# An LSTM step over row pairs as two accumulated Strassen products, in a four-layer graph network

## The chip, the cores and the metric

The kernel runs on one core of one Trainium2 chip. The metric is the device time of one execution in microseconds (us), from the first instruction to the last. Three runs of the kernel before gave 2534.42, 2536.03 and 2541.12 us; the median, 2536.03 us, is the number to compare with.

A core has a matrix engine (TensorE, "PE" in a profile, with its weight loads as "PEld"), a vector engine (VectorE, "DVE"), an engine for activation functions (ScalarE, "ACT"), GpSimd ("POOL"), and SyncE ("SP"), which here only issues transfers. TensorE reads from the on-chip memory SBUF and writes its sums into PSUM, eight banks of 512 fp32 numbers for each of 128 partitions.

## The reference, cut to what matters

The input is 128 small graphs of 64 nodes with 256 features, so 8192 rows of 256 numbers, and one adjacency matrix of 64 x 64. Four graph layers follow one another, each of the form `x = layernorm(x + layer(x, adj))`. All is fp32. Layer 0 has three matrix products with the squared adjacency, layer 1 goes through the eigenvectors of a 64 x 64 matrix, layer 2 is two graph convolutions and then LSTMs along the nodes, layer 3 is attention. Only layer 2's LSTMs are changed:

```python
def step(carry, x_t):
    h, c = carry
    g = x_t @ Wih.T + h @ Whh.T + bias
    i, f, gg, o = jnp.split(g, 4, axis=-1)
    c = sigmoid(f) * c + sigmoid(i) * tanh(gg)
    h = sigmoid(o) * tanh(c)
    return (h, c), None
...
for p in range(1, MAX_SKIP + 1):            # 1, 2, 3, 4
    nw = Tv // p
    wins = h[:, :nw * p, :].reshape(Bv * nw, p, Hd)
    last = _lstm_last(Wih[p-1], Whh[p-1], bih[p-1], bhh[p-1], wins)
    h = h.at[:, arange(nw) * p + (p - 1), :].set(last.reshape(Bv, nw, Hd))
```

For p = 2 each window is a pair of neighbouring nodes. Its first step has a zero state, so only `x_t @ Wih.T` counts. Its second step needs both products: 1024 gate values (four gates of 256) from 256 features of x and 256 of h.

## The kernel before, in words

**Groups.** The 8192 rows are 64 tiles of 128 rows, taken four at a time: 16 groups of 512 rows, which are 8 graphs of 64 nodes. All rows stay in SBUF in one tile `X` (64 KB for each partition).

**Two phases.** In the first phase layer 0 runs over all groups, two at a time, while VectorE works out the eigenvectors (`eigen`) in between. At the end of each group of layer 0 the operations of its normalization are put in a list, `norms`, fourteen for each group; the matrix products of the following group take one from it each (`between`, and the loop over products in `layer0`). In the second phase `group(g)` takes each group through layers 1, 2 and 3 and writes it out; three groups (`WAYS`) are in flight.

**Order.** TensorE's order is written out by hand. Each group is a generator that yields the time at which its next matmul may start, by a clock `now` which adds up matmul costs. The loop at the end takes the oldest group that is due; if none is, it moves the clock on. The wait after a chain on other engines is a constant: after an LSTM step it is `CELL[n]`, 3.8 us for 256 columns. If the chain takes longer in truth, TensorE stands still, since it works strictly in order. The orders of VectorE and ScalarE are chosen by the tile scheduler, and they are kept in order too.

**LSTM steps.** `lstm(hT, p, first, nw)` holds the nodes transposed: `hT` has the 256 features as two halves k of 128 partitions, and as columns node and graph. For p = 2 there are 32 pairs in each of 8 graphs: n = 256 columns. A step makes 8 blocks, gate (f, i, g, o) by half h, each one PSUM bank: two matmuls with the 128 x 128 weight blocks of `wih` for the two k, and two with `whh` for the state `hs`. Each block then goes through a tanh on ScalarE (line 1030; sigmoids are tanh with a scale) to the SBUF tile `gates`. Lines 1034 to 1038 make c, line 1039 tanh(c), line 1041 the state of a step that is not the last, line 1051 the write of the last state into `hT`. In every step but the first, the x part of the first two blocks is given to TensorE ahead of the wait for the state (`early`, `ahead`).

For p = 3 and p = 4 the columns are 168 and 128, so matmuls of 128 columns are already in the kernel; p = 1 is taken in two halves of 256 columns.

**Buffers.** The pool `pw` has five tiles of 1024 columns with the tag "w" for `hT`, the mixed rows and layer 3's tiles; `pv` has four of 512; `psb` has the eight PSUM banks; `pg` holds gates, c and states three times.

Of the kernel before, what the change touches and what calls it, by code (L numbers as in the profile page):

```python
# [10 lines left out]
F32 = mybir.dt.float32  # L11
# [522 lines left out]
P = 128  # L534
# [3 lines left out]
ENDING = (14, 15)  # L538
LEAD = 10


def norm_parts(tc, pool, x, half, scalar=False):

# [53 lines left out]
def kernel(  # L597
# [46 lines left out]
    def load(pool, name, src, pattern, shape, **kw):  # L644
        t = pool.tile(shape, F32, name=name)
        nc.sync.dma_start(t, src.rearrange(pattern, **kw))
        return t

    X = keep.tile([P, NT, D], F32, name="X")
    adst = keep.tile([P, N], F32, name="adst")  # L650
    eig_c = ea.tile([P, len(CONSTS), N], F32, name="eig_c")
    nc.scalar.dma_start(adst[:N, :], adj)
    nc.sync.dma_start(adst[N:, :], adj)
    nc.scalar.dma_start(X[:, 2:4, :], x_t[:, 2:4, :])
    for t in range(2):
        nc.sync.dma_start(X[:, t, :], x_t[:, t, :])
# [6 lines left out]
    for t in range(4, NT, 2):  # L663
        nc.sync.dma_start(X[:, t:t + 2, :], x_t[:, t:t + 2, :])
    nc.sync.dma_start(eig_c, consts)

    ident = keep.tile([P, P], F32, name="ident")
# [74 lines left out]
            yield now[0] + 0.3  # L742

    def layer0(g):
        xs = X[:, 4 * g:4 * g + 4, :]

        def mixed(dst, src, nf, more, then=None):
            for c in range(nf):
# [105 lines left out]
        for t in (2, 0):  # L854
            p = tl(psa, [P, 2, D], "ps", bufs=6)
            mm(p, sqT2, s3[:, t:t + 2, :])
            yield now[0]
            x2 = xs[:, t:t + 2, :]
            VL.tensor_add(x2, p, x2)
            norms.extend(scalar_norm(tc, small, x2, half, spare))  # L860

# [50 lines left out]
    for i in range(4):  # L912
        wih.append(load(wb, f"wih{i}", c_ih[i], "(k p) f -> p k f", [P, 2, 1024], p=P))
        whh.append(load(wb, f"whh{i}", c_hh[i], "(k p) f -> p k f", [P, 2, 1024], p=P) if i else None)
    att = []
    for i in range(WAYS):
        att.append(wb.tile([P, 4, P], F32, name=f"att{i}"))
# [44 lines left out]
    def layer1(xs, ready):  # L962
# [25 lines left out]
            yield now[0]  # L988
        return ready

    def lstm(hT, p, first, nw):

        n = 8 * nw
        wi, wh, bias = wih[p - 1], whh[p - 1], cbi[:, p - 1, :]
        c = hs = None
        for t in range(p):
            rows = slice(first + t, first + t + (nw - 1) * p + 1, p)
            xt = [hT[:, k, rows, :] for k in range(2)]  # L1000
            last = t == p - 1
            names = "figo" if t else "igo"
            G = tl(pg, [P, 2048], "gates")[:, :2 * len(names) * n].rearrange("p (q h n) -> p q h n", h=2, n=n)
# [12 lines left out]
            if p > 1 and not t:  # L1016
                c = tl(pg, [P, 512], "c")[:, :2 * n].rearrange("p (h n) -> p h n", h=2)
            new = None if last else tl(pg, [P, 512], "hs")[:, :2 * n].rearrange("p (h n) -> p h n", h=2)
            for h, q in units:
                j = 2 * "ifgo".index(q) + h  # L1020
                m = slice(j * P, (j + 1) * P)
                pp = ahead.get((h, q))
                if pp is None:
                    pp = ps4()[:, :n]
                    for k in range(2):
                        mm(pp, wi[:, k, m], xt[k], k == 0, k == 1 and not t)
                if t:
# [12 lines left out]
                if q == "o" and not last:  # L1040
                    V.scalar_tensor_tensor(new[:, h, :], gate["o"][:, h, :], 1.0, gate["i"][:, h, :], op0=ALU.add,  # L1041
                                           op1=ALU.mult)
                if q == "o":
                    if h == 0:
                        yield now[0]
                elif h == 1 or len(units) == 8:
                    yield now[0]
            if last:

                for h in range(2):  # L1050
                    V.scalar_tensor_tensor(hT[:, h, slice(first + p - 1, first + nw * p, p), :],  # L1051
                                           gate["o"][:, h, :].rearrange("p (w b) -> p w b", b=8), 1.0,
                                           gate["i"][:, h, :].rearrange("p (w b) -> p w b", b=8), op0=ALU.add,
                                           op1=ALU.mult)
            ready = now[0] + CELL[n]
            hs = new
        return ready

    def layer2(xs, g, ready):
        a = yield from mixed(xs, adT2, ready)  # L1060
        g1 = as3(work(), 4)
        ready = []
        for t in range(0, 4, 2):
            p = ps4((P, 2, D))
            for j in range(2):
                run(p[:, j, :], [(a[:, k, (t + j) * P:(t + j + 1) * P], cw0[:, k, :]) for k in range(2)])
            V.tensor_add(g1[:, t:t + 2, :], p, wide["c_b0"].unsqueeze(1).to_broadcast([P, 2, D]))
            relu(g1[:, t:t + 2, :], g1[:, t:t + 2, :])
            ready.append(now[0] + CONV)
            yield now[0]  # L1070
        a = yield from mixed(g1, adT2, ready)
        hT = tl(pw, [P, 1024], "w").rearrange("p (k n b) -> p k n b", k=2, b=8)
        for c in range(2):
            p = ps4((P, 4, P))
            run(p, [(cw1[:, k, c * P:(c + 1) * P], a[:, k, :]) for k in range(2)])
            h = work2()
            V.scalar_tensor_tensor(as3(h, 4), rs_row.unsqueeze(1).to_broadcast([P, 4, P]), cb1[:, c:c + 1], p,
                                   op0=ALU.mult, op1=ALU.add)
            S.activation(hT[:, c, :, :].rearrange("p n b -> p b n"), as3(h, 8), AF.Relu, scale=2.0)
            yield now[0]  # L1080
        ready = now[0] + CONV
        for p, first, nw in ((1, 0, 32), (1, 32, 32), (2, 0, 32), (3, 0, 21), (4, 0, 16)):
            if first == 0:
                yield ready
            ready = yield from lstm(hT, p, first, nw)
        hb = as3(work(), 2)
        V.tensor_copy(as3(hb[:, 0, :], 8), hT[:, 0, :, :].rearrange("p n b -> p b n"))
        S.copy(as3(hb[:, 1, :], 8), hT[:, 1, :, :].rearrange("p n b -> p b n"))
        yield ready + 1.6
        ready = []  # L1090
        for t in range(0, 4, 2):
            p = ps4((P, 2, D))
            for j in range(2):
                for k in range(2):
                    turn(p[:, j, k * P:(k + 1) * P], hb[:, k, (t + j) * P:(t + j + 1) * P])
            V.scalar_tensor_tensor(xs[:, t:t + 2, :], p, 0.5, xs[:, t:t + 2, :], op0=ALU.mult, op1=ALU.add)  # L1096
            norm(xs, t, ready, 1.8 if t and g in ENDING else 0.0 if g in ENDING else 1.3, scalar=g in ENDING)
            yield now[0]
        return ready
# [85 lines left out]
            yield now[0]  # L1185

    def group(g):
        xs = X[:, 4 * g:4 * g + 4, :]
        ready = [0.0, 0.0]
        ready = yield from layer1(xs, ready)  # L1190
        ready = yield from layer2(xs, g, ready)
# [4 lines left out]
            yield from layer3(xs, g, ready, 0, 2)  # L1196
        else:
            yield from layer3(xs, g, ready, 0, 4)

# [60 lines left out]
```

## Time and profile before

| engine | busy us | share of the span |
|---|---|---|
| TensorE, matmuls | 2494.8 | 98% |
| TensorE, weight loads | 2196.2 | 86% |
| VectorE | 1407.8 | 55% |
| ScalarE | 1090.6 | 43% |
| GpSimd | 134.2 | 5% |

The profiled execution spans 2539.1 us. The first phase takes the first 860 us, the second the rest. Transfers are heavy at the very start (219 GB/s in the first fortieth of the span) and when the second phase's weights come in (117 GB/s), and nearly absent elsewhere.

How to read a profile: a group of instructions stands with its line, its engine, its operation, out<-in tiles and shape, a count, the busy time and the mean of one. Matmuls overlap, so the length of one is longer than its share of the time; what one costs in a dense stretch is the distance from start to start. A line of waits has the waiting engine and tile, the releaser, the total in us, how often, and the longest. A line of a stretch has, for each engine, the busy time and the number of instructions, then the clock share granted to TensorE, the transfer share and GB/s.

### The profile page before, as it was taken

The page shows a single profiled execution, that of the slowest core. Times are in us where ns is not written, and L with a number is a line of the kernel's source. Part 1 is how long each engine was busy: PE and PEld are TensorE (multiplying, and loading weights), DVE is VectorE, ACT ScalarE, POOL GpSimd, SP SyncE. Part 2 cuts the span into 40 slices and gives each one's busy share as a digit, 9 for nine tenths or more (in the row PEclk, how much of TensorE's full clock was granted, in tenths as well). Part 3 has the DMA queues.
Part 4 walks back from the last instruction along what each step waited for, and adds up shares of the span by engine and source line. Part 5 has one row for each costly group of instructions (what it writes and reads, how often), then busy time and mean ns, then how long its engine had stood idle before and what let it go on. Part 6 is the DMA issues. An engine that isn't in the chain of part 4 may idle for free.

```text
span 2539.1 us, 39015 instructions
## 1 busy us (share of the span) xinstructions
PE 2494.8 (98%) x15020; PEld 2196.2 (86%) x15020; DVE 1407.8 (55%) x4996; ACT 1090.6 (43%) x2706; POOL 134.2 (5%) x316
## 2 busy tenths in 40 slices
PE   9999999999999999999999999999999999999997
PEld 7788887888878889998989889898998998978996
DVE  6888777778885433454453543544445345353235
ACT  2344333433333344445344444444444534535454
POOL 0000000000000100000000000000000000010001
PEclk9999999999999999999999999999999999999998
DMA  6000000000000300000000000000000000000000
GB/s 219 1 1 1 1 1 1 1 1 1 1 1 1 117 1 1 10 9 1 9 9 1 9 1 10 9 1 9 1 9 9 1 9 9 1 9 1 1 1 26
DMA packets 24634, 32.09 MB, mean 13 GB/s; under 512 B 2176, under 2 KB 21376, under 8 KB 24448
## 3 DMA queue, kind: packets, MB, share of 16 engines
q1 hardware_dynamic: 24096, 29.32, 3.4%
q8 instruction: 118, 1.93, 0.3%
q14 instruction: 68, 0.56, 0.1%
q10 hardware_dynamic: 352, 0.28, 0.0%
HBM read 21.20 MB, written 8.39 MB: 12 GB/s over the span
## 4 chain that ended last, share of the span: by engine, by line
PE 91%; DVE 5%; POOL 2%; issue 1%; DMA 0%; ACT 0%; SPq 0%; ACTq 0%; POOLq 0%; DVEq 0%
PE ps L716 88%; PE ps L926 2%; POOL ln_rs L554 1%; DVE X L564 1%; DVE ln_st L551 1%; DVE D L51 1%; PE ps L1146 1%; PE pc L93 1%; DMA X<-in_x_dram 0%; POOL ln_rs L553 0%; DVE tw L51 0%; DVE ln_mv L552 0%; DVE X L1176 0%; DVE X L986 0%; DVE X L1096 0%
## 5 line engine op out<-in xcount | busy, mean ns | idle before, releaser
L716 PE MATMUL ps<-w,wih 128*128 128x256 f32 (+2 forms) x4992 | 894.0, 319 | 1.8 <-DVE w L1051 1.8
L716 PEld LDWEIGHTS ps<-w,wih 128*128 128x128 f32 x4992 | 760.9, 191 | 47.8 <-issue 5.7
L1030 ACT ACTIVATE gates<-ps,cbi 128x128 f32<-128x128 f32 (+2 forms) x1248 | 499.3, 410 | 523.3 <-PE ps L716 516.2
L716 PE MATMUL ps<-hs,whh 128*128 128x128 f32 (+2 forms) x3072 | 540.5, 303 | 6.2 <-DVE hs L1041 6.2
L716 PEld LDWEIGHTS ps<-hs,whh 128*128 128x128 f32 x3072 | 453.9, 191 | 32.9 <-issue 11.2
L1036 DVE SCALAR_TENSOR_TENSOR gates<-gates 128x256 f32<-128x256 f32 (+2 forms) x256 | 89.3, 349 | 297.4 <-ACT gates L1030 297.4
L716 PE MATMUL ps<-aw,h 128*128 128x256 f32 x1024 | 227.2, 379 | 0.0
L716 PEld LDWEIGHTS ps<-aw,h 128*128 128x128 f32 x1024 | 192.9, 190 | 25.9 <-ACT h L725 0.5
L725 ACT ACTIVATE h<-h 128x512 f32<-128x512 f32 x128 | 80.5, 629 | 170.0 <-DVE h L51 169.8
L1039 ACT ACTIVATE gates<-c 128x128 f32<-128x128 f32 (+2 forms) x288 | 98.1, 341 | 114.1 <-DVE c L1038 87.9
L1034 DVE SCALAR_TENSOR_TENSOR c<-gates,c 128x128 f32<-128x128 f32 (+2 forms) x192 | 62.6, 326 | 139.4 <-ACT gates L1030 138.2
L1051 DVE SCALAR_TENSOR_TENSOR w<-gates 128x256 f32<-128x256 f32 (+2 forms) x160 | 59.6, 376 | 108.5 <-PE ps L716 73.5
L716 PE MATMUL ps<-ss,tw 128*128 128x256 f32 x512 | 117.9, 380 | 0.0
L716 PE MATMUL ps<-ss,aw 128*128 128x256 f32 x512 | 117.3, 379 | 0.0
L716 PE MATMUL ps<-m,aw 128*128 128x256 f32 x512 | 117.1, 380 | 0.0
L716 PE MATMUL ps<-aw,m 128*128 128x512 f32 x256 | 114.8, 594 | 0.0
L1041 DVE SCALAR_TENSOR_TENSOR hs<-gates 128x128 f32<-128x128 f32 (+2 forms) x192 | 62.6, 326 | 93.6 <-ACT gates L1039 52.4
L553 POOL TENSOR_SCALAR ln_rs<-ln_mv 128x2 f32<-128x2 f32 x96 | 26.2, 273 | 1558.4 <-DVE ln_mv L552 1557.9
L716 PEld LDWEIGHTS ps<-ss,aw 128*128 128x128 f32 x512 | 96.6, 190 | 12.8
L716 PEld LDWEIGHTS ps<-ss,tw 128*128 128x128 f32 x512 | 96.3, 190 | 12.9 <-issue 0.2
L564 DVE TENSOR_SCALAR X<-X,ln_mv,ln_rs 128x256 f32<-128x256 f32 x176 | 64.7, 410 | 75.9 <-POOL ln_rs L554 75.9
L716 PEld LDWEIGHTS ps<-m,aw 128*128 128x128 f32 x512 | 95.6, 190 | 12.6 <-issue 0.5
(294 smaller groups left out, 3107.4 us busy)
## 6 DMA issues: line engine op xcount, KB each, us to landing
X<-in_x_dram SPq DMA_DIRECT2D x30, 256.0 KB, 6.3
out_dram<-X SPq DMA_DIRECT2D x28, 256.0 KB, 2.1
wih<-in_c_ih_dram SPq DMA_DIRECT2D x4, 1024.0 KB, 7.2
aw<-in_a_w_dram SPq DMA_DIRECT2D x3, 1024.0 KB, 10.3
whh<-in_c_hh_dram SPq DMA_DIRECT2D x3, 1024.0 KB, 9.4
out_dram<-X SPq DMA_DIRECT2D x8, 128.0 KB, 1.7
aw<-in_a_w_dram SPq DMA_DIRECT2D x1, 512.0 KB, 5.8
cw<-in_c_w_dram SPq DMA_DIRECT2D x2, 256.0 KB, 5.1
```

The lines of the kernel that those rows point to most:

```text
L51: return getattr(self.engine, name)(out, *args, **kw)
L553: nc.gpsimd.tensor_scalar(rs, mv[:, :, 1], EPS, None, op0=ALU.add)
L564: nc.vector.tensor_scalar(x[:, t, :], x[:, t, :], mv[:, t, 0:1], rs[:, t:t + 1], op0=ALU.subtract, op1=ALU.mult)
L716: PE.matmul(out, lhsT, rhs, start=start, stop=stop)
L725: S.activation(dst, src, AF.Relu)
L926: PE.transpose(out, in_, ident)
L1030: S.activation(gate[q][:, h, :], pp, AF.Tanh, bias=bias[:, j:j + 1], scale=0.5 if q == "g" else 0.25)
L1034: V.scalar_tensor_tensor(c[:, h, :], gate["f"][:, h, :], 1.0, c[:, h, :], op0=ALU.add, op1=ALU.mult)
L1036: V.scalar_tensor_tensor(to, gate["i"][:, h, :], 1.0, gate["g"][:, h, :], op0=ALU.add, op1=ALU.mult)
L1039: S.activation(gate["i"][:, h, :], c[:, h, :] if p > 1 else to, AF.Tanh, scale=0.5)
L1041: V.scalar_tensor_tensor(new[:, h, :], gate["o"][:, h, :], 1.0, gate["i"][:, h, :], op0=ALU.add, op1=ALU.mult)
L1051: V.scalar_tensor_tensor(hT[:, h, slice(first + p - 1, first + nw * p, p), :], gate["o"][:, h, :].rearrange("p (w b) -> p w b", b=8), 1.0, ...
```

## The change: what it does and what it is for

The second step for p = 2 is taken out of the common loop into a function, `second`, and computed by Strassen's scheme in Winograd's form: a product of 2 x 2 blocks by seven block products in place of eight, at the price of block sums. The output's rows are cut into two (b: gates i and g, or f and o), the features into two (k), and the columns into two (the first 16 pairs and the last 16). The x product and the h product add up: they use the same scheme, so each of the seven products is accumulated in PSUM over both sources (s) and summed once. The function does this for each half h, with q for the two gates of a row block. Layer 0 of the kernel already uses the same scheme.

It needs three kinds of sums. Sums of weights (`sums`, four for each source) are made once, by `add_weights`, in the first group. Differences of x and h columns are made for each group, eight operations of 128 columns, in a tile `both` with the tag "w". Sums of products: seven for each h, on VectorE from PSUM into the gates tile, with a copy of the first product by ScalarE. A PSUM bank is taken for two products, which are then summed together. Tanh then reads the gates tile instead of PSUM. After the step the wait is `CELL[256] + 1.0`. Nothing is put ahead of the wait for the state.

The weight sums take 16 KB for each partition. To make room, `X` has twelve groups instead of sixteen. Layer 0 runs over groups 12 to 15 first, in the places of groups 0 to 3; each is then written to DRAM (`rest`), and groups 0 to 3 are loaded in their places (`change`, the last item of the group's entries in `norms`). In the second phase groups 0 to 3 end by loading the rows of groups 12 to 15 into their places.

The core of the diff:

```diff
+LATE = 4
-    X = keep.tile([P, NT, D], F32, name="X")
+    X = keep.tile([P, NT - 4 * LATE, D], F32, name="X")
+    rest = [aside.tile([P, 4, D], F32, name=f"rest{i}") for i in range(LATE)]
+    order = list(range(NT // 4 - LATE, NT // 4)) + list(range(NT // 4 - LATE))
+    def rows_of(g):
+        at = g % (NT // 4 - LATE)
+        return X[:, 4 * at:4 * at + 4, :]
...
     def layer0(g):
-        xs = X[:, 4 * g:4 * g + 4, :]
+        xs = rows_of(order[g])
+        def change():
+            nc.sync.dma_start(rest[g], xs)
+            for t in (0, 2):
+                nc.sync.dma_start(xs[:, t:t + 2, :], given(order[g + LATE])[:, t:t + 2, :])
...
+        if g < LATE:
+            norms.append(change)
...
+    def quarters(w):
+        w = w.rearrange("p k (a b h m) -> p k a b h m", a=2, b=2, h=2)
+        return [w[:, k, :, b] for b in range(2) for k in range(2)]
+    sums = [wb.tile([P, 4, 2, 2, P], F32, name=f"sums{i}") for i in range(2)]
+    ways = [[quarters(w)[i] for i in (0, 1, 3)] + [s[:, i] for i in range(4)]
+            for w, s in zip((wih[1], whh[1]), sums)]
+    def add_weights():
+        for w, s in zip((wih[1], whh[1]), sums):
+            a11, a12, a21, a22 = quarters(w)
+            V.tensor_add(s[:, 0], a21, a22)
+            V.tensor_sub(s[:, 1], s[:, 0], a11)
+            V.tensor_sub(s[:, 2], a11, a21)
+            V.tensor_sub(s[:, 3], a12, s[:, 1])
...
+    def second(hT, xt, hs, G, c, bias, ready):
+        G = G.rearrange("p (h w m q n) -> p h w m q n", h=2, w=2, m=2, q=2)
+        both = tl(pw, [P, 1024], "w").rearrange("p (s i n) -> p s i n", s=2, i=4)
...
+        def less(s, b1, b2, part):
+            T = [both[:, s, i].rearrange("p (w b) -> p w b", b=8) for i in range(4)]
+            if 0 in part:
+                V.tensor_sub(T[0], b1[1], b1[0])
+            if 1 in part:
+                V.tensor_sub(T[2], b2[1], b1[1])
+                V.tensor_sub(T[1], b2[1], T[0])
+                V.tensor_sub(T[3], b2[0], T[1])
...
+        less(0, x1, x2, (0, 1))
+        less(1, h1, h2, (0, 1))
...
+        moving = ((x1[0], h1[0]), (x2[0], h2[0]), (x2[1], h2[1]), T4, T1, T2, T3)
+        weight = (0, 1, 6, 2, 3, 4, 5)
+        yield ready
+        for h in range(2):
+            u1 = work2()[:, :256].rearrange("p (q n) -> p q n", q=2)
+            a, b, c12, d = (G[:, h, w, m] for w in range(2) for m in range(2))
+            def two(*which):
+                p = ps4((P, 2, 2, P))
+                for at, i in enumerate(which):
+                    for q in range(2):
+                        for s in range(2):
+                            mm(p[:, at, q, :], ways[s][weight[i]][:, q, h, :], moving[i][s], s == 0, s == 1)
+                return p[:, 0], p[:, 1]
+            p1, p2 = two(0, 1)
+            S.copy(u1, p1)
+            V.tensor_add(a, u1, p2)
+            yield now[0]
+            p6, p7 = two(5, 6)
+            V.tensor_add(c12, u1, p6)
+            V.tensor_add(b, c12, p7)
+            yield now[0]
+            p5, p3 = two(4, 2)
+            V.tensor_add(d, b, p5)
+            V.tensor_add(c12, c12, p5)
+            V.tensor_add(c12, c12, p3)
+            p4, _ = two(3)
+            V.tensor_add(b, b, p4)
+            gate = {}
+            for m, q, name in ((1, 0, "f"), (0, 0, "i"), (0, 1, "g"), (1, 1, "o")):
+                j = 2 * "ifgo".index(name) + h
+                gate[name] = G[:, h, :, m, q, :]
+                S.activation(gate[name], gate[name], AF.Tanh, bias=bias[:, j:j + 1],
+                             scale=0.5 if name == "g" else 0.25)
...
+        return now[0] + CELL[256] + 1.0
...
+            if p == 2 and t:
+                ready = yield from second(hT, xt, hs, G, c, bias, ready)
+                break
...
             if first == 0:
                 yield ready
+            elif g == 0:
+                add_weights()
...
+        if g < LATE:
+            nc.sync.dma_start(xs, rest[g])
```

The lines left out are the start of the loads in the new order, the views x1, x2, h1, h2 of the column halves, and the gate arithmetic after the tanh, which is as before but for four writes of 128 columns into `hT` in place of two of 256.

More of the change, by code (lines that the diff above doesn't have):

```diff
@@ L647, in load, with given @@
         return t
-    X = keep.tile([P, NT, D], F32, name="X")
+    X = keep.tile([P, NT - 4 * LATE, D], F32, name="X")
+    aside = ctx.enter_context(tc.tile_pool(name="aside", bufs=1, space=bass.MemoryType.DRAM))
+    rest = [aside.tile([P, 4, D], F32, name=f"rest{i}") for i in range(LATE)]
[3 more added lines that the diff above has]
+        return X[:, 4 * at:4 * at + 4, :]
+    def given(g):
+        return x_t[:, 4 * g:4 * g + 4, :]
     adst = keep.tile([P, N], F32, name="adst")
@@ L653 @@
     nc.sync.dma_start(adst[N:, :], adj)
-    nc.scalar.dma_start(X[:, 2:4, :], x_t[:, 2:4, :])
+    nc.scalar.dma_start(rows_of(order[0])[:, 2:4, :], given(order[0])[:, 2:4, :])
     for t in range(2):
-        nc.sync.dma_start(X[:, t, :], x_t[:, t, :])
+        nc.sync.dma_start(rows_of(order[0])[:, t, :], given(order[0])[:, t, :])
     aw1 = load(wa, "aw1", a_w1, "(k p) f -> p k f", [P, 2, 512], p=P)
@@ L662 @@
     aw3 = load(wa, "aw3", a_w3, "(k p) f -> p k f", [P, 8, D], p=P)
-    for t in range(4, NT, 2):
-        nc.sync.dma_start(X[:, t:t + 2, :], x_t[:, t:t + 2, :])
+    for g in order[1:LATE] + order[2 * LATE:]:
+        for t in (0, 2):
+            nc.sync.dma_start(rows_of(g)[:, t:t + 2, :], given(g)[:, t:t + 2, :])
     nc.sync.dma_start(eig_c, consts)
@@ L744, in layer0 @@
     def layer0(g):
-        xs = X[:, 4 * g:4 * g + 4, :]
+        xs = rows_of(order[g])
+        def change():
+            nc.sync.dma_start(rest[g], xs)
+            for t in (0, 2):
+                nc.sync.dma_start(xs[:, t:t + 2, :], given(order[g + LATE])[:, t:t + 2, :])
         def mixed(dst, src, nf, more, then=None):
@@ L989, in layer1, with halves @@
         return ready
+    def second(hT, xt, hs, G, c, bias, ready):
+        G = G.rearrange("p (h w m q n) -> p h w m q n", h=2, w=2, m=2, q=2)
+        both = tl(pw, [P, 1024], "w").rearrange("p (s i n) -> p s i n", s=2, i=4)
+        def halves(b):
+            return b[:, 0:16], b[:, 16:32]
+        def less(s, b1, b2, part):
[6 more added lines that the diff above has]
+                V.tensor_sub(T[3], b2[0], T[1])
+        x1, x2 = (halves(b) for b in xt)
+        h1, h2 = (halves(hs[:, k, :].rearrange("p (w b) -> p w b", b=8)) for k in range(2))
+        less(0, x1, x2, (0, 1))
+        less(1, h1, h2, (0, 1))
+        T1, T2, T3, T4 = ([both[:, s, i].rearrange("p (w b) -> p w b", b=8) for s in range(2)] for i in range(4))
+        moving = ((x1[0], h1[0]), (x2[0], h2[0]), (x2[1], h2[1]), T4, T1, T2, T3)
[31 more added lines that the diff above has]
+                             scale=0.5 if name == "g" else 0.25)
+            ch = c[:, h, :].rearrange("p (w n) -> p w n", w=2)
+            V.scalar_tensor_tensor(ch, gate["f"], 1.0, ch, op0=ALU.add, op1=ALU.mult)
+            V.scalar_tensor_tensor(gate["g"], gate["i"], 1.0, gate["g"], op0=ALU.add, op1=ALU.mult)
+            V.scalar_tensor_tensor(ch, ch, 0.5, gate["g"], op0=ALU.mult, op1=ALU.add)
+            S.activation(gate["i"], ch, AF.Tanh, scale=0.5)
+            yield now[0]
+        for h in range(2):
+            for w in range(2):
+                o, i = (G[:, h, w, m, 0 if m == 0 else 1, :].rearrange("p (w b) -> p w b", b=8) for m in (1, 0))
+                V.scalar_tensor_tensor(hT[:, h, 32 * w + 1:32 * w + 32:2, :], o, 1.0, i, op0=ALU.add, op1=ALU.mult)
+        return now[0] + CELL[256] + 1.0
@@ L1002, in lstm @@
             names = "figo" if t else "igo"
-            G = tl(pg, [P, 2048], "gates")[:, :2 * len(names) * n].rearrange("p (q h n) -> p q h n", h=2, n=n)
+            G = tl(pg, [P, 2048], "gates")
+            if p == 2 and t:
+                ready = yield from second(hT, xt, hs, G, c, bias, ready)
+                break
+            G = G[:, :2 * len(names) * n].rearrange("p (q h n) -> p q h n", h=2, n=n)
             gate = {q: G[:, i] for i, q in enumerate(names)}
@@ L1187, in group @@
     def group(g):
-        xs = X[:, 4 * g:4 * g + 4, :]
+        xs = rows_of(g)
         ready = [0.0, 0.0]
```

## The prediction

> **What bounds the kernel now.** I read the page's busy shares and clock first, then the chain that ended last, then stretches of the steady state, then TensorE's own waits, then the order of instructions around the changed step.
>
> ```profile
> PE 2494.8 (98%) x15020; PEld 2196.2 (86%) x15020; DVE 1407.8 (55%) x4996; ACT 1090.6 (43%) x2706; POOL 134.2 (5%) x316
> ...
> PEclk9999999999999999999999999999999999999998
> ...
> PE 91%; DVE 5%; POOL 2%; issue 1%; DMA 0%; ACT 0%; SPq 0%; ACTq 0%; POOLq 0%; DVEq 0%
> ```
>
> TensorE is busy nearly all the span, at full clock, and is 91% of the chain. A group of four row tiles takes 102.8 us in the steady state (the same place in the pattern comes at 1728.09 and 1933.64 us, two groups apart). The stretches (PE, PEld, DVE, ACT, POOL busy us) show who has room:
>
> ```profile
> 1728.00:1743.00 15.00, 15.00 (x75) 13.32 (x75) 8.15 (x24) 4.94 (x11) 1.98 (x4) 1.00 0.11 37
> 1743.00:1773.00 30.00, 30.00 (x198) 28.18 (x197) 10.17 (x25) 13.41 (x34) 0.00 (x0) 1.00 0.00 1
> ...
> 1100.00:2200.00 1100.00, 1088.07 (x7314) 992.16 (x7313) 506.05 (x1432) 497.97 (x1244) 63.54 (x128) 1.00 0.02 6
> ```
>
> VectorE is 46% busy on the whole (506/1100), but 54% in the first stretch, which is just the second step of a row pair, and 34% in the next. TensorE's waits from 900 to 2380 us:
>
> ```profile
> PE ps L716 <- DVE X L564: 6.9, 5, 2.8
> PE ps L716 <- DVE hs L1041: 5.4, 4, 1.3
> PE ps L716 <- ACT v L725: 3.0, 1, 3.0
> PE ps L716 <- DVE w L1051: 1.8, 2, 1.5
> PE ps L716 <- ACT v L979: 0.7, 1, 0.7
> ```
>
> They sum to 17.8 us in 1480: the due times in the code (CELL and the like) already cover nearly every chain. So only fewer or shorter matmuls, or new waits, can move the time by much.
>
> The unit costs are pitches, start to start, since matmuls overlap. Two pieces of TensorE's timeline (start and length in us), 128 columns and 256 columns:
>
> ```profile
> 1676.24 0.61 PE L716 MATMUL ps<-w,wih 128*128 128x128 f32 x4
> 1676.68 0.61 PE L716 MATMUL ps<-hs,whh 128*128 128x128 f32 x4
> 1677.13 0.61 PE L716 MATMUL ps<-w,wih 128*128 128x128 f32 x4
> ...
> 1732.28 1.03 PE L716 MATMUL ps<-w,wih 128*128 128x256 f32 x4
> 1733.14 1.03 PE L716 MATMUL ps<-hs,whh 128*128 128x256 f32 x4
> 1734.00 1.03 PE L716 MATMUL ps<-w,wih 128*128 128x256 f32 x4
> ```
>
> Four instructions at 256 columns go by in 0.864 us, 0.216 each; at 128 columns in 0.447 us, 0.1117 each (0.447 from 1676.68 on). Every mm() of the code is two instructions in this trace, so it costs 0.432 and 0.2234 us. Halving the columns leaves 52%, not 50%.
>
> [...] the rows of before have 419 (L1150, one operand in PSUM) and 291 (L1034 at 128). [...]
>
> **The change, part by part.**
>
> *Matmuls.* Before, the second step has 8 gate blocks of 2+2 mm at 256 columns: 32 x 0.432 = 13.82 us a group. After, for each h seven products, each 2 (q) x 2 (s) mm at 128 columns: 56 x 0.2234 = 12.51 us. Saved 1.31 us a group, x16 = **21.0 us**, all on TensorE, which is the path. I take the pitch of the p = 4 steps for the new matmuls, since these also change weights every mm and alternate two sources.
>
> *VectorE.* Removed: two 256-column writes of hT (0.84). Added a group: 8 differences of 128 columns (x 0.29 = 2.3), 14 sums of 256 columns (x 0.42 = 5.9), four writes of 128 columns in place of the two (1.16). The three gate operations per h remain. Net 8.5 us a group: from 46% to some 55% of a period, no bound on average. ScalarE gets two copies more (at about 0.4 us as the tanh on 256 elements from SBUF), and its tanh reads SBUF instead of PSUM (0.41 for 0.47): about nothing.
>
> *Local VectorE load.* In 1728 to 1743 us VectorE has 8.15 us of work, of which the step's own is seven operations of 0.42, 2.9; the rest is the old group's closing norm. With 8.5 more it is 16.6 us for a stretch of 13.7. Two parts can lie outside: the four x differences before `ready`, and the closing 2.8 us (one sum, three gate operations, the hT writes) after the last matmul, where VectorE was a third busy. That leaves about 12.6 in 13.7: full, with a lag of perhaps 0.5 us. PSUM has 8 banks and the step fills one in 1.8 us, so such a lag reaches no matmul through a bank.
>
> *The wait after the step.* The first step of p = 3 cannot start until hT is written. Chain after the last matmul: sum 0.42, three tanh at 0.33 pitch to the end of the third 1.1, two VectorE operations 0.9, tanh 0.42, two writes 0.6, handovers about 0.4: 3.85 us, against 1.45 before (1742.64 to 1744.09). The due time goes from 3.8 to 4.8. Room shrinks from 2.35 to 0.95 us, less the 0.5 of lag. Bounds: 0, or about 1 us a group if lag doubles. I take 0.2, **+3 us** in all.
>
> *No matmuls ahead.* Before, two gate blocks' x parts (4 mm, 1.73 us) were put ahead of `ready`. Now nothing is, so other groups must fill 1.7 + 1.0 us more a group. In the steady state they have about 28 us of other work and the next group's first step. At the end, with groups 14 and 15 alone, it may show: 0 to 4 us, I take **+1**. First differences on h stand ahead of nothing: the first two products use raw x and h, 1.8 us, and T2 needs only three differences (0.9).
>
> *Rows in DRAM.* Layer 0 takes groups 12 to 15 first. Row set 0's last normalization ran by 101 us; its swap is the 15th item of the list, so it comes out at the third row set's first product, about 127 us, and the fifth set's rows are read at 178. Between lie 512 KB out and two 256 KB loads, 10 to 17 us by the rows 2.1 and 6.3 us. The fourth swap slips to about 293 for a read at about 340. In the second phase the rows come back some nine groups ahead of use. SyncE waits there, and behind it are only outputs. Nothing. `add_weights` is eight operations of 128x512 (0.69 each), 5.5 us on VectorE once, during the second half of the first group's p = 1 step; all weights have been issued by 861 and that step starts near 904. 0 to 3 us, I take **+1**.
>
> Work pool: `both` takes a fifth of the "w" buffers during the step. Counting live tiles at 1720 to 1743 (hT, both, hn, one mixed) gives four or five of five: just enough.
>
> Sum: -21 + 3 + 1 + 1 = **-16**, 2536 to **2520 us**.
>
> **Rivals.** (A) *VectorE lag eats it.* For: 16.6 us of demand in a 13.7 us stretch, and a chain of seven handovers whose room is 0.95 us. Against: the load falls to a third right after, and the other groups can fill. If each group waits about 1.2 us, 16 x 1.2 = 19 of 21 us go: **2534**. (B) *The order breaks up*: late VectorE work also delays the other groups' copies and norms, whose own due times are unchanged, or a "w" buffer is missing. Single waits of 2.8 and 3.0 us stand in the trace. One of 2.8 a group costs 45: 2536 - 21 + 45 = **2560**, slower. Against: the waits of before are 17.8 us in all although other stretches too are dense (6.53 of 8 us on VectorE at 1842 to 1850, with one wait of 1.0 beside it). (C) *More than counted*: the reordering also clears some of the 17.8 us of waits: **2511**.
>
> **Chances.** Forecast 0.62 (2512 to 2528), C 0.06, A 0.16 (2529 to 2543), B 0.16. Faster by over 0.3% (under 2528.4): 0.68; within: 0.16; slower: 0.16. The range from 2510 to 2546 leaves out most of B and the far end of C.
>
> **What would show it.** TensorE's instructions rise by 1792 - 1024 = 768, to 15788; its 128-column pitch in the step is 0.1117. VectorE's busy time goes to about 1408 + 136 + 5 = 1550. The group period falls from 102.8 to about 101.6. If A, TensorE waits on the hT writes of the new step, about 1 us a group; if B, on norms, copies or differences of `both`. I would be wrong if the 128-column matmuls with their semaphore waits go by slower than 0.1117, since 7% more pitch (0.120) takes 15 us of the 21.

## The result and the profile after

The changed kernel takes 2581.32 us (median of 4 runs, 2579.39 to 2584.46) against 2536.32 (the three runs of before and a fourth): a ratio of 1.0176, with a 95% interval from 1.0158 to 1.0194. The forecast was 2520, its range 2510 to 2546. It is slower by 45 us where 16 us faster was forecast.

The page of the changed kernel, the same lines as before:

```profile
PE 2489.7 (97%) x15788; PEld 2209.6 (86%) x15788; DVE 1520.7 (59%) x5388; ACT 1098.5 (43%) x2738; POOL 140.2 (5%) x316
...
PEclk9999999999999999999999999999999999999999
...
PE 81%; DVE 12%; POOL 3%; ACT 2%; issue 2%; DMA 0%; SPq 0%; ACTq 0%; POOLq 0%; DVEq 0%
```

The count of matmuls is the forecast one (15788). The row of nines does not mean a full clock all through, since a nine stands for 90% or more: the mean granted clock of the changed kernel's runs is 0.991 to 0.992, and that of the kernel before 0.993 in runs of 2539 to 2542 us and 0.995 or 0.996 in runs of 2534 to 2537 us (more below). VectorE has gone from 5% to 12% of the chain that ended last, and ScalarE from nothing to 2%. TensorE's waits from 940 to 2400 us (releaser; total us, how often, longest):

```profile
PE ps L731 <- DVE w L1104: 20.0, 9, 2.2
PE ps L731 <- DVE w L1171: 15.1, 10, 1.5
PE ps L731 <- DVE w L997: 9.4, 10, 1.9
PE ps L731 <- ACT v L1023: 9.1, 12, 1.4
PE ps L731 <- DVE hs L1161: 4.9, 1, 4.9
```

With two small ones (1.3 and 0.7 us) they sum to 60.5 us, against 17.8 before. L1104 is the new step's write of `hT`. L1171 (formerly L1051) is the same write for the other p, here after p = 1, since all who wait for it are matmuls of 256 columns, L997 the copy of mixed rows, L1023 layer 1's copy, L1161 the state of a step. So a third of the waiting is just behind the new step; the other two thirds are at places whose code the diff does not touch.

The steady state now repeats every group: the p = 3 step resumes at 1669.66 and again at 1776.28 us, 106.6 us apart, where it was 102.8. Stretches of the changed kernel, the new step, the 10 us after it, and the steady state:

```profile
1750.00:1767.00 17.00, 16.98 (x164) 16.32 (x164) 13.71 (x39) 4.04 (x11) 1.50 (x4) 1.00 0.00 1
1767.00:1777.00 10.00, 6.94 (x51) 6.28 (x50) 8.02 (x22) 3.94 (x9) 1.26 (x3) 1.00 0.16 53
1100.00:2200.00 1100.00, 1045.98 (x7522) 963.18 (x7521) 560.73 (x1645) 481.31 (x1206) 60.97 (x130) 0.99 0.02 8
```

VectorE (the third engine of a line) is 81% busy in the step and 80% in the 10 us after it; in the 10 us after the old step, in the kernel before, it was 38%:

```profile
1743.00:1753.00 10.00, 10.00 (x70) 9.61 (x69) 3.83 (x8) 4.71 (x12) 0.00 (x0) 1.00 0.00 0
```

TensorE stands 3.1 of the changed kernel's 10 us. Its two stops there, and then what VectorE did meanwhile:

```profile
1766.97 0.39 PE L731 MATMUL ps<-w,whh 128*128 128x128 f32 x2
1767.20 1.95 PE L731 MATMUL ps<-adT,X 128*128 128x128 f32 x16
1768.98 1.95 PE L731 MATMUL ps<-u,X 128*128 128x128 f32 x16
1771.77 1.99 PE L731 MATMUL ps<-cw,w 128*128 128x256 f32 x8 [0.84 <-DVE w L997]
1773.60 0.45 PE L731 MATMUL ps<-w,wih 128*128 128x168 f32 x2
1776.28 6.22 PE L731 MATMUL ps<-w,wih 128*128 128x168 f32 x30 [2.22 <-DVE w L1104]
1782.33 1.89 PE L731 MATMUL ps<-cw,w 128*128 128x256 f32 x8
```

```profile
1768.77 0.39 DVE L1084 TENSOR_TENSOR gates<-gates,ps 128x256 f32<-128x256 f32 x1
1769.08 0.18 DVE L554 BATCH_NORM_AGGREGATE ln_mv<-ln_st 128x2 f32<-128x6 f32 x1
1769.17 0.39 DVE L1085 TENSOR_TENSOR gates<-gates,ps 128x256 f32<-128x256 f32 x1
1770.38 0.74 DVE L566 TENSOR_SCALAR X<-X,ln_mv,ln_rs 128x256 f32<-128x256 f32 x2 [0.82 <-POOL ln_rs L556]
1771.03 0.69 DVE L997 COPY w<-ps 128x512 f32<-128x512 f32 x1
1771.63 0.41 DVE L1086 TENSOR_TENSOR gates<-gates,ps 128x256 f32<-128x256 f32 x1
1771.96 0.41 DVE L1088 TENSOR_TENSOR gates<-gates,ps 128x256 f32<-128x256 f32 x1
1772.29 0.68 DVE L1009 TENSOR_TENSOR X<-X,wide_b_b 128x512 f32<-128x512 f32 x1
1772.89 0.68 DVE L997 COPY w<-ps 128x512 f32<-128x512 f32 x1
...
1775.73 0.49 DVE L1104 SCALAR_TENSOR_TENSOR w<-gates 128x128 f32<-128x128 f32 x2
```

The step's last matmul pair starts at 1766.97 and passes by 1767.2. The sums of its last two banks are L1084 to L1088. Between these and the write of `hT` VectorE, in its fixed order, does another group's norm (and stands 0.82 us there for GpSimd), copies mixed rows and adds a bias. The trace shows that order: L1086 reads a bank whose matmuls were over by 1767.4 and the sums of L1085, over at 1769.56, yet it starts at 1771.63, behind the 0.82 us of standing, the norm and a copy. TensorE keeps its order in the same way: the eight matmuls of 1782.33 read the mixed rows that those of 1771.77 had read, and not `hT`, and yet they start only behind the 30 that had to wait for `hT` until 1776.28. `hT` is complete at 1776.2, 9.0 us after the last matmul.

**Half clock.** The granted clock of the changed kernel falls to 0.5 six times between 1000 and 2400 us, for 3.4 us each; matmuls of 168 columns follow each other every 0.280 us there (56 distances, median) in place of 0.1425, those of 256 every 0.427 in place of 0.216. One fall lies just behind the stop of 2.22 us above:

```profile
1777.30:1780.60 3.30, 3.30 (x14) 3.30 (x13) 0.67 (x2) 1.43 (x4) 0.00 (x0) 0.50 0.00 0
```

The 30 instructions of 168 columns from 1776.28 on take 6.05 us from start to start, where 30 pitches of 0.1425 are 4.3. TensorE has no recorded wait in these six stretches but works at these pitches, about half speed, so they cost some 10 us (half of 6 x 3.4) which no list of waits shows. Each fall begins within 1.3 us after the end of a recorded wait of 1.9 us or more; there are eleven such waits, so five of them had none. e10 has no wait above 1.4 us in that stretch and no fall. So falls came with long waits here; that the waits bring them is my reading of these traces, and no run tested it by itself.

**A budget for all runs.** A recorded wait understates what TensorE loses, since the drawn length of a matmul (0.275 us at 128 columns, where the pitch is 0.112) covers the first part of the pause behind it. So I add up the pitches of all matmul instructions (0.429 us at 512 columns, 0.216, 0.1425 at 168, 0.1117 at 128, and at 64 columns 0.037, where the groups of 32 in the changed kernel take 0.035: under 1 us over the span) and take the sum from the distance between the first and the last start: what is left, TensorE stood or went slower than these pitches, the half clock included. Times are medians; the other columns are of one profiled execution, which lies up to 5 us from the median (that of before was its slowest, 2541 us), so that a difference of standing under 5 us says nothing. The last column is the time between 1000 and 2400 us that the clock was at half; the loss is about half of it.

| kernel | time us | matmuls need | TensorE stands or is slow | clock at half |
|---|---|---|---|---|
| before | 2536.3 | 2467.4 | 60.4 | 10.2 |
| changed | 2581.3 | 2446.4 | 120.9 | 20.5 |
| e1_rows_only | 2538.0 | 2467.4 | 57.9 | 10.2 |
| e2_no_sums | 2540.2 | 2446.4 | 80.5 | 3.4 |
| e3_prio | 2549.1 | 2446.4 | 91.0 | 3.4 |
| e4_due4 | 2556.0 | 2446.4 | 96.8 | 20.5 |
| e5_lstm_prio | 2528.4 | 2446.4 | 68.1 | 0 |
| e6_before_prio | 2530.2 | 2467.4 | 47.8 | 6.8 |
| e7_order_only | 2547.4 | 2467.4 | 64.7 | 0 |
| e8_prio_due2p5 | 2520.9 | 2446.4 | 60.4 | 6.8 |
| e9_due2p5 | 2537.7 | 2446.4 | 74.1 | 6.8 |
| e10_lstm_prio_due2p5 | 2512.8 | 2446.4 | 53.1 | 0 |
| e11_before_load | 2548.6 | 2467.4 | 69.4 | 17.1 |
| e12_before_prio_due | 2523.0 | 2467.4 | 43.1 | 0 |
| e13_load_prio | 2543.3 | 2467.4 | 64.0 | 20.5 |
| e14_lstm_prio_due4 | 2545.2 | 2446.4 | 85.6 | 13.7 |
| e15_diff_pool | 2511.5 | 2446.4 | 51.2 | 0 |

By this sum the seven products need the forecast 21.0 us less. That is counts times pitches and no measurement by itself; what is measured is that the matmuls of the new step do follow each other every 0.112 us (the median of their distances). The changed kernel stands or is slow 60.5 us more for them. (That this equals the 60.5 us of recorded waits above is chance.)

### The profile page after: what moved, and what is told of

Read it like the earlier page. It is cut to its first block, busy times and chain, and to the rows that moved or that the text cites. A ratio compares the mean times of both kernels' runs of the same rounds, so it can differ in the third digit from the quotient of the medians.

```text
span 2578.3 us, 41027 instructions
## 1 busy us (share of the span) xinstructions
PE 2489.7 (97%) x15788; PEld 2209.6 (86%) x15788; DVE 1520.7 (59%) x5388; ACT 1098.5 (43%) x2738; POOL 140.2 (5%) x316
## 4 chain that ended last, share of the span: by engine, by line
PE 81%; DVE 12%; POOL 3%; ACT 2%; issue 2%; DMA 0%; SPq 0%; ACTq 0%; POOLq 0%; DVEq 0%
PE ps L731 79%; POOL ln_rs L556 2%; DVE X L566 2%; DVE ln_st L553 2%; PE ps L970 1%; ACT gates L1093 1%; DVE D L51 1%; POOL ln_rs L555 1%; DVE ln_mv L554 1%; DVE X L1218 1%; PE pc L93 1%; DVE w L1262 0%; DMA X<-in_x_dram 0%; DVE w L997 0%; DVE X L1009 0%
## 5 line engine op out<-in xcount | busy, mean ns | idle before, releaser
L731 PE MATMUL ps<-w,wih 128*128 128x128 f32 (+2 forms) x4864 | 849.4, 311 | 35.8 <-DVE w L1104 20.0
L731 PEld LDWEIGHTS ps<-w,wih 128*128 128x128 f32 x4864 | 731.1, 193 | 75.7 <-DVE w L1104 22.3
L1150 ACT ACTIVATE gates<-ps,cbi 128x128 f32<-128x128 f32 (+2 forms) x1120 | 441.6, 403 | 451.6 <-PE ps L731 445.3
L731 PE MATMUL ps<-hs,whh 128*128 128x128 f32 (+1 forms) x2816 | 459.3, 287 | 5.8 <-DVE hs L1161 5.8
L731 PEld LDWEIGHTS ps<-hs,whh 128*128 128x128 f32 x2816 | 397.1, 192 | 9.1 <-DVE hs L1161 6.1
L1156 DVE SCALAR_TENSOR_TENSOR gates<-gates 128x128 f32<-128x128 f32 (+2 forms) x224 | 75.9, 339 | 245.2 <-ACT gates L1150 245.1
L740 ACT ACTIVATE h<-h 128x512 f32<-128x512 f32 x128 | 80.5, 629 | 184.1 <-DVE h L51 183.9
L1161 DVE SCALAR_TENSOR_TENSOR hs<-gates 128x128 f32<-128x128 f32 (+2 forms) x192 | 62.7, 327 | 94.5 <-ACT gates L1159 59.5
L731 PE MATMUL ps<-w,sums 128*128 128x128 f32 x896 | 114.0, 276 | 0.0
L1159 ACT ACTIVATE gates<-c 128x128 f32<-128x128 f32 (+2 forms) x256 | 84.5, 331 | 62.8 <-DVE c L1158 48.1
L566 DVE TENSOR_SCALAR X<-X,ln_mv,ln_rs 128x256 f32<-128x256 f32 x176 | 64.7, 410 | 78.0 <-POOL ln_rs L556 78.0
L731 PEld LDWEIGHTS ps<-w,sums 128*128 128x128 f32 x896 | 107.4, 192 | 1.7 <-issue 0.5
L1154 DVE SCALAR_TENSOR_TENSOR c<-gates,c 128x128 f32<-128x128 f32 (+1 forms) x160 | 49.2, 308 | 100.7 <-ACT gates L1150 100.1
L731 PEld LDWEIGHTS ps<-ss,tw 128*128 128x128 f32 x512 | 96.3, 190 | 12.9 <-issue 0.2
```

Source lines behind the costliest of these rows:

```text
L566: nc.vector.tensor_scalar(x[:, t, :], x[:, t, :], mv[:, t, 0:1], rs[:, t:t + 1], op0=ALU.subtract, op1=ALU.mult)
L731: PE.matmul(out, lhsT, rhs, start=start, stop=stop)
L740: S.activation(dst, src, AF.Relu)
```

## The experiments

My theory after the result: VectorE's sums come late because VectorE keeps its order, and the new TensorE order makes other chains meet badly too. Rivals: VectorE's load by itself; the moved rows; slow products.

**Rows alone.** e1 has the change without `second`, `sums` and `add_weights`.

> The rows of four groups wait in DRAM and layer 0 takes groups 12 to 15 first, but the second step for p = 2 is the old one: no weight sums, no seven products. Lag theory (VectorE's work in the new step comes too late and TensorE waits): within 0.3% of before, 2529 to 2544 us. Rival (moving the rows costs): 2550 us or more, with TensorE waits on transfers or a later start of groups 12 to 15.

Measured 2537.96 us, ratio 1.0004 (0.9995 to 1.0013). Moving the rows costs nothing that can be measured.

**Sums left out.**

```diff
-            S.copy(u1, p1)
-            V.tensor_add(a, u1, p2)
...
...
-                S.activation(gate[name], gate[name], AF.Tanh, bias=bias[:, j:j + 1],
+                S.activation(gate[name], banks[name][:, :, q, :], AF.Tanh, bias=bias[:, j:j + 1],
```

> As the changed kernel, TensorE's order unchanged to the matmul, but the 14 sums of products and two copies of each group are left out: the four tanh of an h read single products from PSUM, so the gates are not those of the reference. Lag theory: TensorE's waits on the writes of hT after the step (20 us) and on the mixed rows (9 us) go, the waits at other places (hT after p = 1, 15 us; layer 1's copies, 9 us) stay since the order makes them: about 2550 us. Sheer load theory (all waits come from 8 us more VectorE work a group): all of them go, 2515 to 2525 us. If the seven products themselves were slow: still over 2570.

Measured 2540.18 us, ratio 1.0010 (1.0001 to 1.0018): 41 us faster than the changed kernel, and still not faster than before. Its waits from 1000 to 2400 us:

```profile
PE ps L731 <- DVE w L1165: 15.1, 10, 1.5
PE ps L731 <- ACT v L1023: 8.0, 12, 1.0
PE ps L731 <- DVE hs L1155: 4.8, 1, 4.8
```

The wait after the new step is gone, half of the one on mixed rows too (4.7 us are left). The 15.1 us after p = 1 (line L1165 here, the former L1171) and the waits on L1023 and on the state stand to a tenth or so as they were, though VectorE is relieved. TensorE's order is the same in both traces, matmul for matmul, so they come with that order and not with the sums (e5 below shows that VectorE's order has a part too). Sheer load as the cause of all waits has fallen: it would have given 2515 to 2525. Slow products have fallen too.

**Sums first on VectorE.** In `second`, sums, tanh, gate arithmetic and the writes of `hT` are put in `with tc.high_priority(offset=1500):`, as the kernel already does for mixed rows.

> As the changed kernel, with the same results, but the scheduler is told to put the sums, the tanh, the gate arithmetic and the writes of hT of the new step ahead of other groups' work on VectorE and ScalarE. Lag by order (the old group's adds and norms stand ahead of the step's sums): the 20 us of waits on the writes of hT fall under 5, the time to 2555 to 2565. Sheer load: the work is the same, the waits only move to the norms and copies pushed back, 2575 to 2590.

Measured 2549.10 us, ratio 1.0044 (1.0029 to 1.0059), 32 us less than the changed kernel with the same work. The wait on the step's write falls from 20.0 to 4.6 us (ten of at most 0.5); the one on mixed rows from 9.4 to 1.1. The others stay:

```profile
PE ps L731 <- DVE w L1177: 15.1, 10, 1.5
PE ps L731 <- ACT v L1023: 9.1, 12, 1.4
PE ps L731 <- DVE hs L1167: 4.9, 1, 4.9
PE ps L731 <- DVE w L1110: 4.6, 10, 0.5
```

So what stood in the sums' way on VectorE was much of the loss, more than I expected (2555 to 2565). The recorded waits between 1000 and 2400 us fall by 24 us, and the time at half clock from 20.5 to 3.4 us, worth some 8 us more, which I had not reckoned with.

**A longer wait after the step.**

```diff
-        return now[0] + CELL[256] + 1.0
+        return now[0] + CELL[256] + 4.0
```

> As the changed kernel, with the same results, but the wait after the new step is CELL + 4.0 instead of CELL + 1.0 us, so other groups' matmuls come first. Lag theory: the 20 us of waits after the step go, 2555 to 2565 us, if the new order makes no other waits. Order theory (the waits come from which groups' chains meet, and this shifts): anywhere from 2530 to 2590, with the waits at other places than before changed by more than 10 us.

Measured 2555.97 us, ratio 1.0070 (1.0055 to 1.0085). The wait on L1104 falls from 20.0 to 1.3 us and the one after p = 1 is no longer in the list; but new ones appear, 13.5 us on L997, 12.9 on L1245 (layer 3's first copy) and 5.8 on norms (L566). The expectations of both theories hold the time; the moved waits speak for the order.

**All LSTM steps first.** In `lstm` too, each unit's tanh and gate arithmetic and the writes of the state get the same priority.

> As e3_prio, with the same results and TensorE's order the same, and now every LSTM step's tanh, gate arithmetic and state writes are put ahead of other groups' work by the scheduler, so that norms which wait for GpSimd no longer stand ahead of them on VectorE. Theory (order plus VectorE kept in order makes the waits outside the new step): the 15 us of waits on hT after p = 1 and the 5 us on the state go, with what they hide 20 to 25 us: 2525 to 2532 us, faster than before. Rival (the waits only move to the norms and copies pushed back): 2540 to 2555.

Measured 2528.39 us, ratio 0.9962 (0.9949 to 0.9975). The 15.1 and 4.9 us are gone from the list; layer 1's copies (9.2 us) and the step's own write (4.6) stay. In the changed kernel VectorE stands 0.81 and 0.90 us for GpSimd in two norms (1736.81 and 1738.90) just ahead of such a write at 1739.56, for which TensorE waits 1.51. So the waits after p = 1 needed both: a TensorE order in which that step meets other groups' norms, and a VectorE order in which those norms, with their stops for GpSimd, stand ahead.

**The control.** e6 is the kernel before with that priority.

> The kernel before with the same priority on all LSTM steps and nothing else: the control for e5_lstm_prio. Theory: its waits on states are only 7 us in all, so 2528 to 2538 us. Rival (priority is a gain of its own, whatever the step): under 2520.

Measured 2530.24 us, ratio 0.9968 (0.9956 to 0.9980). Priority helps the old kernel by 6 us, so of e5's lead of 8 us over before only about 2 are left for the new step.

**The two changes of order alone.**

```diff
-            early = units[:2] if t else []
+            early = units[:2] if t and p != 2 else []
...
-            ready = now[0] + CELL[n]
+            ready = now[0] + CELL[n] + (1.0 if p == 2 and t else 0.0)
```

> The kernel before, old second step with its 32 matmuls of 256 columns, but without the matmuls ahead of the state and with the wait of CELL + 1.0 after the step: only the two changes of TensorE's order that come with the new step. Theory (a good part of the loss is the order): 2545 to 2570 us, with new waits on hT after p = 1 or on layer 1's copies. Rival (only the sums' lag costs): 2533 to 2543.

Measured 2547.39 us, ratio 1.0038 (1.0024 to 1.0053): 11 us lost with the old matmuls and no sums. The waits are those of the changed kernel in small: `hT` after p = 1 (all who wait for L1051 here are matmuls of 256 columns), layer 1's copies.

```profile
PE ps L716 <- DVE w L1051: 10.6, 7, 1.5
PE ps L716 <- ACT v L979: 5.0, 8, 0.7
```

**Another length of the wait, with and without priority.** e8 is e3 with `CELL[256] + 2.5`, e9 the changed kernel with it.

> As e3_prio, with the same results, but CELL + 2.5 us after the new step. If only the length of that wait matters: the 5 us of waits on hT left after the step go, 2543 to 2547 us. If the order is what counts: the waits on hT after p = 1 (15 us) and on layer 1's copies (9 us) change by more than 10 us together, either way, and the time lies anywhere from 2525 to 2565.

> As the changed kernel, with the same results and the scheduler's own order on VectorE, but CELL + 2.5 us after the new step: TensorE's order is that of e8_prio_due2p5. If the order alone made the gain of e8: 2520 to 2530 us. If priority and order are both needed: 2540 to 2560, with waits on the writes of hT after the step or on the mixed rows of 10 us or more.

e8 took 2520.90 us, ratio 0.9934 (0.9919 to 0.9949); e9 2537.72, ratio 1.0000 (0.9991 to 1.0009). In e8 the wait after p = 1 is not in the list any more and the one on L1023 is 2.4 us: together 22 us less than in e3, so the order counts; the time is below both expectations. e9 lies between its two expectations. A change of 1.5 us in one constant is worth 44 us on the changed kernel and 28 with the sums first; 17 us lie between e9 and e8, which have one TensorE order, matmul for matmul, and differ in VectorE's and ScalarE's.

**Both mends, and their control.** e10 is e5 with `CELL[256] + 2.5`; e12 is e6 with 2.5 us more after the old second step.

> Both mends together, with the same results: priority on all LSTM steps (e5) and CELL + 2.5 us after the new step (e8). Theory: the 5 us of wait on a state that e8 has left go too, 2512 to 2519 us, the fastest. Rival (the priority of the other steps only pushes norms back): 2519 to 2526, no better than e8.

> The kernel before with e5's priority on all LSTM steps and CELL + 2.5 us after the second step for p = 2: the old matmuls with the same two mends, the control for e10. If the new step's 21 us of saved matmuls are real once the waits are out: 15 to 22 us above e10, 2530 to 2540. If the mends alone make e10's gain: within 5 us of e10.

e10 took 2512.79 us, ratio 0.9899 (0.9883 to 0.9916), a version faster than both kernels. Its two largest waits from 1000 to 2400 us:

```profile
PE ps L731 <- ACT v L740: 2.5, 10, 0.3
PE ps L731 <- ACT v L1023: 2.4, 2, 1.4
```

The control e12 took 2522.99 us, ratio 0.9940 (0.9925 to 0.9955), 10.2 us above e10; I had expected 15 to 22. Of e10's gain of 24 us, 14 belong to the mends, which the old step can have as well, and 10 to the new step: its 21.0 us of saved matmuls less 10.0 us more standing (53.1 against 43.1). This holds at this one due time: the old step was not run at others with priority, and it keeps its matmuls ahead of the state, so the two TensorE orders are not the same.

**VectorE's load by itself.** e11 is the kernel before with idle work in each of the eight blocks of the second step:

```diff
+                if p == 2 and t:
+                    for _ in range(2):
+                        V.tensor_add(idle, wide["d_b"][:, :192], pp[:, :192])
+                    V.tensor_sub(idle[:, :128], wide["d_b"][:, :128], wide["d_b"][:, 128:])
```

> The kernel before with its results unchanged, and in the second step for p = 2 of each group 24 idle VectorE operations whose results nobody reads: 16 sums of 192 columns with an operand in PSUM and 8 differences of 128, by the rows some 8 us a group, as much as the new step adds, but in no chain. Sheer load theory: VectorE's work by itself costs 15 us or more, 2552 us and up. Theory (what costs is that the sums lie in the chain and in a fixed order): 2536 to 2546.

> The kernel before with e5's priority on all LSTM steps (that alone: 2530 us) and e11's 24 idle VectorE operations in each group's second step, which have no priority. Results unchanged. If e11's 12 us came from the idle work standing ahead of the chain on VectorE: they vanish, 2527 to 2534 us. If VectorE's load costs by itself wherever it stands: 2538 us and up.

e11 took 2548.61 us, ratio 1.0041 (1.0026 to 1.0056), between the two expectations; its largest wait is 14.2 us on the write of `hT`, 12.7 of it behind the second step for p = 2. e13 took 2543.31, ratio 1.0018 (1.0008 to 1.0028), 13 us above e6. The wait on `hT` is gone there, but TensorE now waits 14.9 us on norms (L564) in place of e6's 7.3. So my theory was wrong on this point: the load, whose results nobody reads, costs 12 to 13 us in either VectorE order, and priority only chooses where TensorE stands. Both runs also spend more time at half clock than before and e6 (17.1 and 20.5 us against 10.2 and 6.8), which is a part of this. The idle sums also read the block's PSUM bank, but no wait on a bank is in the lists.

**Is the length of the wait still a lottery with priority on?**

> As e10, with the same results, but CELL + 4.0 us after the new step. If, with priority on, a longer wait only has to be long enough: 2509 to 2517 us, as e10. If each length gives another meeting of chains whatever the priority: outside 2505 to 2520, with waits at other places than e10's.

Measured 2545.24 us, ratio 1.0028 (1.0018 to 1.0039): 32 us above e10 for 1.5 us more of wait, the same instructions otherwise. TensorE stands on mixed rows and norms instead:

```profile
PE ps L731 <- DVE w L997: 14.1, 11, 2.7
PE ps L970 <- DVE X L566: 7.8, 14, 1.3
```

**Differences on GpSimd.** In `less`, `V.tensor_sub` becomes `nc.gpsimd.tensor_sub`.

> As e10, with the same results, but the eight differences of x and h columns are made on GpSimd instead of VectorE (2.3 us a group off VectorE). If VectorE's load is what is left of the loss (some 10 us): 2505 to 2510 us. If the differences lie in the start of the step's chain and GpSimd is slower: 2515 to 2530, with TensorE waiting on the tile of differences.

Measured 2511.53 us, ratio 0.9896 (0.9881 to 0.9911), between the two expectations, and the ranges of e10 and e15 overlap. The differences are not where the remaining 10 us lie.

## Why the prediction was wrong, step by step

*Matmuls: right.* 15788 instructions, the pitch of 0.1117 (pairs at 1750.05, 1750.27 and 1750.49 us), 21.0 us saved by count and pitch. What sets this pitch no run shows.

*Rows in DRAM, bank and "w" buffers: right.* e1 shows the first. No wait on a PSUM bank or on the differences is in the list.

*VectorE's sum: oversized.* Busy time rose by 113 us to 1520.7, not to 1550. The drawn lengths do rise by 142 us, as I had added them up, but operations in a row overlap: two sums start 0.33 us apart (1771.63 and 1771.96) though each is drawn 0.41 long. My prices were such drawn lengths, from rows of before: 0.419 us at 256 columns (L1150, one operand in PSUM) and 0.291 at 128 (L1034).

*The wait after the step: the step that failed first.* I priced the chain at 3.85 us with 0.5 of lag, counting VectorE as "a third busy" behind the step. It was 80% busy there and the chain took 9.0 us. I had put the step's own closing work into a stretch that I knew from before, without asking which other work the shifted order would bring there: mixed rows, a bias, a norm. TensorE was back at 1773.9 (two pitches after 1773.60) and stood 2.4 us, where I had taken 0.2 a group; in all 20.0 us are recorded at this place where I had taken 3. With the sums first (e3) the longest recorded wait is 0.5.

*No matmuls ahead, and a longer due time: the second failure.* I took +1 us in all, thinking that other groups fill in. They do fill in, but this moves every group against the others. That alone cost 11 us with the old matmuls (e7), and e2, with the new ones and no sums, stands 20 us more than before (80.5 against 60.4).

*The clock: put at nothing.* I read the row of nines as full clock and had no term for it. Half clock cost the changed kernel some 10 us between 1000 and 2400 us. The execution of before that I had read has a fall of 10.2 us too, at 2259, beside its waits of 2.8 and 3.0 us.

Rival B named the mechanism (late VectorE work and other groups' chains, with unchanged due times) and gave 2560 from 2.8 us a group; the recorded waits come to 60.5/16 = 3.8. It did not name the half clock. I gave it 0.16 because the waits of before were small. But small waits with constant due times show that the constants fit this one order, not that there is room in them.

What is not settled: how the 60.5 us of standing divide. Leaving out the sums takes 40 of it, putting them first takes 30, moving the due time by 1.5 us takes 47; these overlap, since each also changes which chains meet and how long the clock is at half. Why a given order is good could not be read from any single number; I only measured orders. The remaining 10 us of e10 against e12 were not traced either, beyond that the differences are not the cause; 3.6 of them are recorded waits (7.5 against 3.9 us between 1000 and 2400), and neither has half clock there.

## What to carry to other kernels

When one engine runs in an order fixed by constant due times and stands for almost nothing, saved work on it can be lost to the other engines' queues (here 21.0 us saved came with 60.5 us more of standing): check what stands ahead of the new operations in their queues, in the stretch where they will fall after the change. Give the operations that the fixed engine waits for priority, and try a few values of the due time with and without the change before judging it; here one constant moved the same work by 44 us, twice the gain sought. Measure the control with the same mends, or a schedule's gain is booked to the arithmetic.

## What the runs showed of the hardware that was not expected

The matmul timeline hides part of each pause: the two matmuls that start at 1773.60 are drawn until 1774.05 but take two pitches, until 1773.89, so the pause behind them is 2.39 us long and recorded as 2.22. In the changed kernel the waits recorded sum to 80.4 us over the span, where the pitches leave 120.9. About 15 us of the difference is half clock, some 10 are such hidden parts of the recorded waits, and the rest is in small pieces that I did not sort.

Half clock came beside short waits: falls of 3.4 us to a granted clock of 0.5 right behind waits of 1.9 to 4.9 us, six in the changed kernel, four of them behind waits of 2.2.

VectorE's sums of 256 fp32 columns with an operand in PSUM follow each other every 0.33 us in the changed kernel where the second does not read what the first wrote (0.330 for 23 pairs of L1084 and L1085, 0.329 for 17 of L1086 and L1088; medians of the pairs that stand next to each other), though the profile draws each 0.41 us long, so a load worked out from drawn lengths is a quarter too high for them. Where the second does read it, the distance is 0.45 us (18 pairs of L1080 and L1081, as at 1763.40 and 1763.85, and 8 of L1085 and L1086).
